# Exchanging the two arms of a run-time branch at the end of a two-layer decoder kernel

## The chip, the core and the metric

The kernel runs on one core of a Trainium2 chip. A core has five engines, each with a queue of its own instructions: TensorE (PE: matrix products; its weight loads are shown as PEld), VectorE (DVE), ScalarE (ACT), GpSimd (POOL) and SyncE (SP), which here only issues transfers. A queue is worked off in order by a sequencer; engines wait for each other by semaphores. Sequencer work (branches, semaphore steps, register moves) is listed in the profile under the engine's name with a "q" behind it (SPq, DVEq). 16 DMA engines move data between the device's main memory and the on-chip memory, and also the instructions themselves.

The metric is the time of one execution in device microseconds, as the median of several. A profiled execution also gives the span, from the first to the last instruction of the program.

## The reference

Two decoder layers over x of 4 batches x 256 tokens x 256 features in float32, each sublayer followed by a residual sum and a layer norm:

```python
x = _layernorm(x + _L0_attn_ref(x, ...))    # sliding-window attention, 16 heads
x = _layernorm(x + _L0_xattn_ref(x, ...))   # attention to 1601 context rows
x = _layernorm(x + _L0_ffn_ref(x, ...))     # ternary weights, quantised activations
x = _layernorm(x + _L1_attn_ref(x, ...))    # causal attention, 16 heads
x = _layernorm(x + _L1_xattn_ref(x, ...))   # linear attention, gated
x = _layernorm(x + _L1_ffn_ref(x, ...))     # 2 of 8 experts for each token
```

The change lies behind the last of them. Each token goes to 2 of 8 experts, and the result is a weighted sum:

```python
weights = probs * mask          # softmax of 8 logits, the two largest kept
for e in range(E):
    h = jax.nn.silu(x @ w1[e]) * (x @ w3[e])
    out = out + h @ w2[e] * weights[:, e:e + 1]
```

and the last step of the program is the layer norm of x plus that sum.

## The kernel before

The whole program is written as a list of operations, each with the tiles it reads and writes; a planner (`weave`) orders them by estimated times and due places, and then emits them into the queues. The line numbers that profiles show are therefore mostly those of helpers: L408 emits every operation of VectorE, ScalarE and GpSimd, L271 and L278 the products and transposes, L285 the plain transfers, L1290 the scatters.

**The expert tiles.** Tokens are sorted into lists by expert at run time, padded to tiles of 128 rows. How many tiles there are depends on the data. `tile_table` computes which expert and which rows a tile has. Some tiles are worked early, while the last batch is still in its attention. The rest, `LATE` of them, come at the end: the first `LATE - RARE` always run, and the last `RARE` = 3 only if the lists are so unevenly filled that more tiles are in use. `tile_table` writes this as a number of 0 or 1 to the tile `more` (L1423), which each engine's sequencer loads into a register (L1547).

**The end of the usual path.** The last tiles that always run add their result for each batch to four accumulators `acc` in PSUM, by a product with a selection matrix `pick`; VectorE adds the results of earlier tiles, read back from `yd` in main memory into tiles `back`, to x (`entry`), and a product with the identity adds this to `acc`. Then `finish` makes the layer norm. For each batch of 256 tokens (two groups of 128 rows): VectorE's bn_stats and bn_aggr for mean and variance (`st`, `mv2`); GpSimd's two small operations for the inverse root (`rstd2`); VectorE's `nmr`; VectorE normalises the first group into `back`, ScalarE the second with one Identity activation; SP stores both to `out`. So four activations of ScalarE and four stores of 256 KB end the usual path.

**The rare branch.** After that, `rare_tiles` emits one `tc.Switch` over all five engines. Its flag is `more`. Arm 0 has no work of its own; arm 1 works the three rare tiles, adds them to `acc`, and calls `finish` again, which writes all of `out` once more. In the program every engine's queue holds, in this order: its last usual instruction; the steps of the switch (register moves and a branch that takes its distance from a register, L1722); arm 0; arm 1; the closing block. Each arm begins with a hint that names its exit (BRANCH_PREFETCH_HINT, L1548) and ends with an unconditional branch to the closing block. The framework counts semaphores up through the whole program, so an arm also holds steps that bring each engine's and each DMA lane's semaphore to the value that the other arm would leave. Such a step first waits for the value that the lane has when all its own transfers have landed, and then adds the difference. In arm 0 these are nine on SP (eight DMA lanes and one for its sequencer), two on PE, one each on the others.

**The closing block** (L1722 too, as the line of `weave` in the caller). SP makes twelve semaphore steps of two waits each, which together wait for every semaphore of the program: four steps for the scatters' lanes, eight for the plain transfers' lanes in turn, each with an engine's semaphore as the second. Then it drains and gives its sign. The other engines drain and give theirs; GpSimd counts four signs, releases all, clears the semaphores, and a second round of signs ends the program.

With the inputs of the reference the flag `more` is 0: the usual arm is taken.

Of the kernel before, what the change touches and what calls it, by code (L numbers as in the profile page):

```python
# [23 lines left out]
F32 = mybir.dt.float32  # L24
BF16 = mybir.dt.bfloat16
U32 = mybir.dt.uint32
I32 = mybir.dt.int32
AF = mybir.ActivationFunctionType
ALU = mybir.AluOpType
AX = mybir.AxisListType  # L30

P = 128
B, S, D = 4, 256, 256
T = B * S
# [6 lines left out]
NE, EI = 8, 512  # L41
# [144 lines left out]
class Loom:  # L186
# [79 lines left out]
    def mm(self, o, lhsT, rhs, start, stop, **kw):  # L266
        fns, outs, ins = self.cur
        outs.append(o)
        ins += [v for v in (lhsT, rhs) if isinstance(v, View)]
        fns.append(  # L270
            lambda: self.nc.tensor.matmul(real(o), real(lhsT), real(rhs), start=real(start), stop=stop, **kw)  # L271
        )
# [162 lines left out]
def decoder(ctx: ExitStack, tc: tile.TileContext, a: dict, out: bass.AP):  # L435
    nc = tc.nc
    k = Loom(tc)
# [33 lines left out]
    p5, p5w = linear.pool("p5", 2), linear.pool("p5w")  # L471
# [3 lines left out]
    p6 = work.pool("p6", 3)  # L475

    def bank(shape=(P, 512), dtype=F32, acc=False):
        return psB.tile(shape, dtype, "bank", free=True, acc=acc)

    def tiny(shape, tag, dtype=F32):  # L480
        return small.tile(shape, dtype, tag, free=True)
# [21 lines left out]
    def at_prio(*prio):  # L503
        k.prio = prio
# [106 lines left out]
    vs = []  # L611
    for i in range(2):
        v = p1w.tile((P, 3, H // 2, 2, 32), F32, f"v{i}")
# [624 lines left out]
    LATE = TILES - sum(EARLY)  # L1238
    LAST_TILES = 2
    RARE = NE // 2 - 1  # L1240
# [138 lines left out]
    def tile_table(n, before, last=False):  # L1379


        iotaN, start, nxt = state[4:]
        tag = len(tables)

        def some(w, name):
            return p5.tile((P, w), F32, f"{name}{tag}", bufs=1)

        nt = some(NE, "nt")
        k.vector.tensor_scalar(nt, nxt, 1.0 / P, (127.0 if last else -127.0) / 256.0, ALU.mult, ALU.add)
        k.vector.tensor_scalar(nt, nt, MAGIC, MAGIC, ALU.add, ALU.subtract)  # L1390
        st = start
        if before is not None:
            st = some(NE + 1, "st")
            k.vector.tensor_copy(st, start)
            k.vector.tensor_tensor(st[:, :NE], st[:, :NE], before, ALU.add)
        k.vector.tensor_tensor(nt, nt, st[:, :NE], ALU.subtract)
        upto = some(NE, "upto")
        k.vector.tensor_copy(upto, nt)
        for e in range(1, NE):
            k.vector.tensor_tensor(upto[:, e : e + 1], upto[:, e : e + 1], upto[:, e - 1 : e], ALU.add)  # L1400

        step = some(NE, "step")
        k.vector.tensor_tensor(step, st[:, 1:], st[:, :NE], ALU.subtract)
        k.vector.tensor_tensor(step, step, nt, ALU.subtract)
        past = p5.tile((P, n, NE), F32, f"past{tag}", bufs=1)
        k.vector.tensor_tensor(
            past,
            upto.unsqueeze(1).to_broadcast([P, n, NE]),
            iotaN[:, :n].unsqueeze(2).to_broadcast([P, n, NE]),
            ALU.is_le,  # L1410
        )
        ex, row = some(n, "ex"), some(n, "rowt")
        k.vector.reduce_sum(ex, past, axis=AX.X)
        k.vector.tensor_tensor(past, past, step.unsqueeze(1).to_broadcast([P, n, NE]), ALU.mult)
        k.vector.reduce_sum(row, past, axis=AX.X)
        k.vector.scalar_tensor_tensor(row, row, st[:, 0:1], iotaN[:, :n], ALU.add, ALU.add)
        tab = p5.tile((P, 2, n), I32, f"tab{tag}", bufs=1)
        k.vector.tensor_scalar(tab[:, 0], ex, float(NE - 1), None, ALU.min)
        k.vector.tensor_scalar(tab[:, 1], row, float(P), None, ALU.mult)
        tables.append(tab)  # L1420
        if last:
            more = p5.tile((P, 1), I32, "more", bufs=1)
            k.vector.tensor_scalar(more, upto[:, NE - 1 :], n - RARE + 0.5, None, ALU.is_gt)  # L1423
            return tab, more

        taken = some(NE, "taken")
        k.vector.tensor_tensor(taken, nt, upto, ALU.subtract)
        k.vector.tensor_scalar(taken, taken, float(n), 0.0, ALU.add, ALU.max)
        k.vector.tensor_tensor(taken, taken, nt, ALU.min)
        if before is not None:  # L1430
            k.vector.tensor_tensor(taken, taken, before, ALU.add)
        return tab, taken
# [78 lines left out]
        k.vector.tensor_tensor(slots, slots, slot, ALU.add)  # L1511
        scatter(yd, slots, y, 1.0, 2.0, "give", cleared)

    def finish(acc):

        for b in range(B):
            mv = tiny((P, 2, 2), "mv2")
            o = p6.tile((P, 2, D), F32, "back", bufs=4)
            for t in range(2):
                st = tiny((P, 6), "st")  # L1520
                k.vector.bn_stats(st, acc[b][:, t, :])
                k.vector.bn_aggr(mv[:, t, :], st)
            rstd = tiny((P, 2), "rstd2")
            k.gpsimd.tensor_scalar(rstd, mv[:, :, 1], 1e-5, None, ALU.add)
            k.gpsimd.tensor_tensor(rstd, rstd, mhalf, ALU.pow)
            nmr = tiny((P, 1), "nmr")
            k.vector.scalar_tensor_tensor(nmr, mv[:, 1, 0:1], -1.0, rstd[:, 1:2], ALU.mult, ALU.mult)
            k.vector.tensor_scalar(o[:, 0], acc[b][:, 0], mv[:, 0, 0:1], rstd[:, 0:1], ALU.subtract, ALU.mult)
            k.scalar.activation(o[:, 1], acc[b][:, 1], AF.Identity, scale=rstd[:, 1:2], bias=nmr)
            k.dma_start(out[b * S : (b + 1) * S, :].rearrange("(t p) d -> p t d", p=P), o)  # L1530

    def rare_tiles(tiles, tab, more, level, acc):

        spare = {}
        for v in (
            p5.tile((P, W), F32, "xg"), p6w.tile((P, 2, 2, EI), F32, "wt"), p6.tile((P, 2, P), F32, "xgT"),
            p6.tile((P, EI // P, P), F32, "eh"), p6.tile((P, D), F32, "ey"), p5.tile((P, 1), F32, "of", bufs=2),
            p6.tile((P, T // P, P), F32, "pick", bufs=LAST_TILES), p6.tile((P, 2, D), F32, "back", bufs=4),
            tiny((P, 2, 2), "mv2"), tiny((P, 6), "st"), tiny((P, 2), "rstd2"), tiny((P, 1), "nmr"),
            bank((P, 2, P)), bank((P, EI // P, P)), bank((P, EI // P, P)), bank((P, D)),  # L1540
        ):
            spare.setdefault(v.buf.group.tag, []).append(v)

        def emit():
            k.hold_order(False)
            engines = (nc.tensor, nc.vector, nc.scalar, nc.gpsimd, nc.sync)
            which = {e.engine: e.value_load(more.real()[0:1, 0:1], min_val=0, max_val=1) for e in engines}  # L1547
            for arm in tc.Switch(which, 2):  # L1548
                if arm:
                    for i in tiles:  # L1550
                        k.at_once = spare
                        expert_tile(i, tab, level, acc)
                    finish(acc)
                    k.at_once = None
            k.hold_order(True)

        k.op({None: (0.0, 2.5, emit)}, [*acc], [tab, more, w2], [v for vs in spare.values() for v in vs], after=[o for o in k.ops if o.bufs], unordered=True)


    for b in range(B):  # L1560
# [40 lines left out]
    state, taken = moe_prepare(), None  # L1601
# [4 lines left out]
    w2 = p6w.tile((P, NE, 4, D), F32, "w2e")  # L1606
    for e in range(NE):
        k.dma_start(w2[:, e], rows(a["w2"][e]))
    level = 0
    for b in range(B):  # L1610
        at_prio(7, b)
        for ts, x, xt in l1_attention(b):
            at_prio(6, b)
            if ts[0] == 0:
                entry, xnt = new_entry(), new_xt()
                xn = entry[:, :, 0, :D]
            l1_cross(b, ts, x, xt, xn, xnt)
            if b == B - 1:
                at_prio(8)
                n = EARLY[ts[0]]  # L1620
                tab, taken = tile_table(n, taken)
                for i in range(n):
                    expert_tile(i, tab, level)
            at_prio(6, b)
            route(b, ts, entry, xnt, level)
            level += 1
            at_prio(7, b)
        X[b] = xn
    at_prio(8)
    tab, more = tile_table(LATE, taken, True)  # L1630
    iotaT = p6.tile((P, T), F32, "iotaT", bufs=1)
    iota(iotaT, 1, base=1)
    acc = [bank((P, 2, D)) for _ in range(B)]
    sure = LATE - RARE
    for i in range(sure):
# [5 lines left out]
        if last == 0:  # L1641
            for b in range(B):
# [6 lines left out]
                with piece(0.87, what="base"):  # L1649
                    for t in range(2):  # L1650
                        mm(acc[b][:, t, :], ident, x[:, t, :], False, True, skip_group_check=True)
    finish(acc)
    rare_tiles(range(sure, LATE), tab, more, level, acc)
    k.weave()


# [69 lines left out]
```

## Time and profile before

| what | value |
|---|---|
| median of 3 runs | 690.63 us (690.26 to 690.64) |
| the profiled execution's own time | 690.3 us |
| its span | 688.6 us |
| mean granted clock of TensorE | 0.985 |
| PE busy | 656.5 us (95% of the span) |
| DVE, ACT, POOL busy | 444.0, 296.2, 120.7 us |
| last product of TensorE ends | 675.0 us |
| last instruction of ScalarE | 678.88 us, 0.56 us long |
| stores of `out` issued | four, 675.4 to 679.5 us |
| their time from issue to landing | 3.2 / 4.1 / 4.5 us (least, median, most) |
| instruction packets of the DMA queues | 38 (0.62 MB) on q8, 37 (0.30 MB) on q14 |

Times within the profile count from the start of the span. The table says that TensorE is busy nearly all the time up to 675 us, and that some 13 us of the span lie behind its last product.

### The profile page before, as it was taken

The page shows a single profiled execution, that of the slowest core. Times are in us where ns is not written, and L with a number is a line of the kernel's source. Part 1 is how long each engine was busy: PE and PEld are TensorE (multiplying, and loading weights), DVE is VectorE, ACT ScalarE, POOL GpSimd, SP SyncE. Part 2 cuts the span into 40 slices and gives each one's busy share as a digit, 9 for nine tenths or more (in the row PEclk, how much of TensorE's full clock was granted, in tenths as well). Part 3 has the DMA queues.
Part 4 walks back from the last instruction along what each step waited for, and adds up shares of the span by engine and source line. Part 5 has one row for each costly group of instructions (what it writes and reads, how often), then busy time and mean ns, then how long its engine had stood idle before and what let it go on. Part 6 is the DMA issues. An engine that isn't in the chain of part 4 may idle for free.

```text
span 688.6 us, 12316 instructions
## 1 busy us (share of the span) xinstructions
PE 656.5 (95%) x4385; PEld 524.3 (76%) x4389; DVE 444.0 (64%) x1152; ACT 296.2 (43%) x930; POOL 120.7 (18%) x166
## 2 busy tenths in 40 slices
PE   9999999999999999999989999999997899999992
PEld 6778788678877777777667677777765799899991
DVE  6899887433526844464699997777688466434353
ACT  4779766211132423334347777656445312111101
POOL 3331132122300000000022101141203213121102
PEclk9999999999999999999999999999999899999996
DMA  9932121537998422000010340000000582895432
GB/s 307 363 96 63 45 66 40 177 100 236 335 340 307 146 96 96 0 1 1 1 54 1 105 142 1 1 32 1 31 1 21 207 277 73 295 339 217 146 130 69
DMA packets 62463, 85.36 MB, mean 124 GB/s; under 512 B 4462, under 2 KB 45812, under 8 KB 62388
## 3 DMA queue, kind: packets, MB, share of 16 engines
q1 hardware_dynamic: 60756, 79.96, 34.9%
q0 software_dynamic: 1632, 4.48, 1.8%
q8 instruction: 38, 0.62, 0.4%
q14 instruction: 37, 0.30, 0.1%
HBM read 67.29 MB, written 17.13 MB: 123 GB/s over the span
## 4 chain that ended last, share of the span: by engine, by line
PE 83%; DVE 10%; ACT 4%; POOL 1%; issue 1%; ACTq 0%; POOLq 0%; DVEq 0%
PE bank L271 74%; PE bank L278 9%; ACT at L408 3%; DVE at L408 2%; DVE nm L408 2%; DVE x L408 1%; POOL rstd L408 1%; DVE st L408 0%; DVE h L408 0%; DVE fm L408 0%; DVE as L408 0%; DVE kf L408 0%; ACT fm L408 0%; DVE back L408 0%; DVE bank L408 0%
## 5 line engine op out<-in xcount | busy, mean ns | idle before, releaser
L408 ACT ACTIVATE at<-at,nm 128x128 f32<-128x128 f32 (+1 forms) x256 | 106.4, 419 | 22.6 <-DVE nm L408 21.7
L271 PE MATMUL bank<-xgT,wt 128*128 128x128 f32 x640 | 75.9, 280 | 0.6 <-DVE xgT L408 0.5
L271 PEld LDWEIGHTS bank<-xgT,wt 128*128 128x128 f32 x640 | 75.2, 196 | 1.7 <-DVE xgT L408 0.8
L278 PE MATMUL bank<-ident,at 128*128 128x128 f32 (+1 forms) x440 | 61.4, 277 | 2.0 <-DVE at L408 1.8
L278 PEld LDWEIGHTS bank<-ident,at 128*128 128x128 f32 (+1 forms) x440 | 50.7, 142 | 14.2 <-issue 7.1
L271 PE MATMUL bank<-V,aT 128*128 128x256 f32 (+1 forms) x240 | 55.1, 380 | 0.6 <-DVE o L408 0.6
L271 PE MATMUL bank<-KT,qT 128*128 128x512 f32 (+1 forms) x128 | 54.7, 554 | 0.0
L271 PEld LDWEIGHTS bank<-V,aT 128*128 128x128 f32 (+1 forms) x240 | 45.3, 190 | 10.5 <-issue 3.6
L271 PE MATMUL bank<-kf,V 128*128 128x256 f32 (+1 forms) x208 | 50.0, 382 | 1.1 <-DVE kf L408 1.1
L408 POOL TENSOR_SCALAR rstd<-mv 128x2 f32<-128x2 f32 (+1 forms) x26 | 5.8, 222 | 258.5 <-DVE mv L408 186.2
L408 DVE TENSOR_REDUCE nm<-at 128x4 f32<-128x512 f32 (+1 forms) x64 | 50.6, 809 | 0.4
L271 PE MATMUL bank<-wkv,KT 128*128 128x256 f32 (+1 forms) x208 | 49.6, 382 | 0.0
L408 ACT ACTIVATION_READ_ACCUMULATOR at<-at,nm 128x1 f32 x256 | 48.6, 190 | 0.0
L271 PEld LDWEIGHTS bank<-kf,V 128*128 128x128 f32 (+1 forms) x208 | 38.6, 190 | 7.2 <-DVE kf L408 2.3
L271 PEld LDWEIGHTS bank<-wkv,KT 128*128 128x128 f32 (+1 forms) x208 | 38.0, 186 | 6.9 <-issue 1.0
L408 ACT COPY aT<-bank 128x512 f32<-128x512 f32 (+2 forms) x58 | 30.6, 554 | 26.6 <-PE bank L278 25.8
L408 ACT ACTIVATE eh<-bank 128x512 f32<-128x512 f32 x20 | 11.9, 597 | 66.5 <-PE bank L271 66.5
L408 DVE TENSOR_REDUCE m<-bank 128x1 f32<-128x512 f32 (+1 forms) x32 | 20.5, 640 | 29.7 <-PE bank L271 29.7
L408 DVE TENSOR_TENSOR at<-at,rs 128x512 f32<-128x512 f32 (+1 forms) x44 | 38.4, 873 | 1.0
L408 POOL TENSOR_TENSOR at<-at,rs 128x512 f32<-128x512 f32 (+1 forms) x20 | 22.8, 1141 | 87.9 <-DVE rs L408 80.7
L408 ACT ACTIVATE fm<-bank 128x512 f32<-128x512 f32 (+2 forms) x33 | 17.8, 550 | 46.6 <-PE bank L271 46.1
L271 PE MATMUL bank<-w2e,eh 128*128 x160 | 37.8, 380 | 0.0
(268 smaller groups left out, 1243.2 us busy)
## 6 DMA issues: line engine op xcount, KB each, us to landing
wt<-in_w SPq DMA_DIRECT2D x40, 512.0 KB, 5.0
lists<-h SPq DMA_DIRECT2D x6, 1548.0 KB, 17.9
KT<-in_ctxT SPq DMA_DIRECT2D x6, 1024.0 KB, 6.9
V<-in_ctx SPq DMA_DIRECT2D x6, 1024.0 KB, 6.0
w2e<-in_w SPq DMA_DIRECT2D x8, 512.0 KB, 8.7
KT<-in_ctxT SPq DMA_DIRECT2D x6, 577.0 KB, 5.1
V<-in_ctx SPq DMA_DIRECT2D x6, 512.0 KB, 4.2
xg<-lists SPq DMA_DIRECT2D x20, 129.0 KB, 4.2
```

The lines of the kernel that those rows point to most:

```text
L271: lambda: self.nc.tensor.matmul(real(o), real(lhsT), real(rhs), start=real(start), stop=stop, **kw)
L278: fns.append(lambda: self.nc.tensor.transpose(real(o), real(x), real(ident)))
L408: return getattr(engine, method)(*[real(x) for x in args], **{k: real(x) for k, x in kw.items()})
```

## The change

The flag is turned round: `enough` is 1 where the tiles that always run suffice. `finish` is split in two. `norms` has what VectorE and GpSimd do, and runs ahead of the switch as before; `leave` has the four activations of ScalarE and the four stores. The switch's arm 0 now holds the three rare tiles, then `norms` and `leave` again; arm 1, which stands last and directly ahead of the closing block, holds only `leave`. The rare arm writes the same tiles `back`, `rstd2` and `nmr` that the usual path has filled (entered in `spare`, but no longer claimed as places of their own), and the operation of the switch names them as written. The list of engines in the switch has another order.

```diff
         if last:
-            more = p5.tile((P, 1), I32, "more", bufs=1)
-            k.vector.tensor_scalar(more, upto[:, NE - 1 :], n - RARE + 0.5, None, ALU.is_gt)
-            return tab, more
+            enough = p5.tile((P, 1), I32, "enough", bufs=1)
+            k.vector.tensor_scalar(enough, upto[:, NE - 1 :], n - RARE + 0.5, None, ALU.is_lt)
+            return tab, enough
...
-    def finish(acc):
+    def norms(acc):
+        parts = []
         for b in range(B):
             mv = tiny((P, 2, 2), "mv2")
-            o = p6.tile((P, 2, D), F32, "back", bufs=4)
...
+            o = p6.tile((P, 2, D), F32, "back", bufs=4)
             k.vector.tensor_scalar(o[:, 0], acc[b][:, 0], mv[:, 0, 0:1], rstd[:, 0:1], ALU.subtract, ALU.mult)
+            parts.append((o, rstd, nmr))
+        return parts
+
+    def leave(acc, parts):
+        for b, (o, rstd, nmr) in enumerate(parts):
             k.scalar.activation(o[:, 1], acc[b][:, 1], AF.Identity, scale=rstd[:, 1:2], bias=nmr)
             k.dma_start(out[b * S : (b + 1) * S, :].rearrange("(t p) d -> p t d", p=P), o)

-    def rare_tiles(tiles, tab, more, level, acc):
+    def end(tiles, tab, enough, level, acc, parts):
...
+        held = [v for vs in spare.values() for v in vs]
+        for vs in parts:
+            for v, tag in zip(vs, ("back", "rstd2", "nmr")):
+                spare.setdefault(tag, []).append(v)

         def emit():
             k.hold_order(False)
-            engines = (nc.tensor, nc.vector, nc.scalar, nc.gpsimd, nc.sync)
-            which = {e.engine: e.value_load(more.real()[0:1, 0:1], min_val=0, max_val=1) for e in engines}
+            engines = (nc.tensor, nc.vector, nc.gpsimd, nc.sync, nc.scalar)
+            which = {e.engine: e.value_load(enough.real()[0:1, 0:1], min_val=0, max_val=1) for e in engines}
             for arm in tc.Switch(which, 2):
+                k.at_once = spare
                 if arm:
+                    leave(acc, parts)
+                else:
                     for i in tiles:
-                        k.at_once = spare
                         expert_tile(i, tab, level, acc)
-                    finish(acc)
-                    k.at_once = None
+                    leave(acc, norms(acc))
+                k.at_once = None
             k.hold_order(True)
...
-    finish(acc)
-    rare_tiles(range(sure, LATE), tab, more, level, acc)
+    end(range(sure, LATE), tab, enough, level, acc, norms(acc))
     k.weave()
```

In the built program the order of VectorE's, GpSimd's and TensorE's instructions ahead of the switch is the same as before. On ScalarE the switch follows the last activation of the expert tiles, on SP the eighth load of `back`. In the usual arm SP's queue has: the hint; for each of the four stores a step that brings its DMA lane forward, and the store; then five more steps (its sequencer and the four other lanes); the branch to the closing block. ScalarE's has the hint, the four activations with the steps that wait for their inputs, and the branch. VectorE, GpSimd and TensorE have in it what they had in arm 0 before. The rare arm has 57 instructions on VectorE and 117 (118 before) on TensorE, each product counted once.

## The prediction

> **What bounds the kernel now.** I read the page first, its span and its chain.
>
> ```profile
> span 688.6 us, 12316 instructions
> ...
> PE 83%; DVE 10%; ACT 4%; POOL 1%; issue 1%; ACTq 0%; POOLq 0%; DVEq 0%
> ```
>
> TensorE sets nearly everything, but the change touches only what follows its last product. So I read next the timeline of the last stretch. Columns: start, duration, engine, line, operation.
>
> ```profile
> 673.11 1.89 PE L271 MATMUL bank<-ey,pick 128*128 128x256 f32 x8
> 675.41 4.44 SPq L285 DMA_DIRECT2D out<-back  x4
> 678.26 0.54 DVE L408 TENSOR_SCALAR back<-bank,mv,rstd 128x256 f32<-128x256 f32 x1
> 678.88 0.56 ACT L408 ACTIVATE back<-bank,nmr,rstd 128x256 f32<-128x256 f32 x1 [0.42 <-DVE back L408]
> ```
>
> The products end at 675.0, ScalarE's last activation at 679.44, the fourth store is issued at 679.47. The span ends at 688.6: 9.1 us in which no engine computes. What fills them is in the rows of the switch (L1722, the closing block included) and of its first arm (L1548). First and last start stand behind the durations in ns.
>
> ```profile
> L1722 SPq EVENT_SEMAPHORE  x14: 17/28/28, 686.9 to 688.5; - x14
> ...
> L1722 POOLq DRAIN  x3: 40/112/2933, 681.2 to 688.3; - x3
> ...
> L1722 PEldq COMPARE_BRANCH  x2: 351/2010/3670, 672.2 to 675.3; - x2
> ...
> L1722 POOLq COMPARE_BRANCH  x2: 43/52/60, 677.6 to 678.3; - x2
> ...
> L1722 DVEq COMPARE_BRANCH  x2: 60/68/75, 678.4 to 679.2; - x2
> ...
> L1722 ACTq COMPARE_BRANCH  x2: 43/50/58, 679.1 to 679.7; - x2
> ...
> L1722 SPq COMPARE_BRANCH  x2: 42/50/58, 680.1 to 684.2; - x2
> L1722 DVEq DRAIN  x2: 10/29/48, 684.1 to 688.0; - x2
> L1722 ACTq DRAIN  x2: 8/44/80, 684.4 to 688.0; - x2
> ```
>
> Each queue branches twice: at the switch, into arm 0, which stands right behind; and out of arm 0, past the rare arm, to the closing block. SP's second branch is at 684.2 and its first closing semaphore step at 686.9: 2.7 us with nothing done. DVE's takes 679.2 to 684.1, 4.9 us; ACT's 679.7 to 684.4, 4.7; POOL's 678.3 to 681.2, 2.9; PE's 3.67 by its own duration. The first branch costs little: on DVE 678.4 to the arm's first record at 679.0, 0.6.
>
> Why SP leaves so late stands in the rows of arm 0 and in the waits of SP's queue (line, releaser, us in total, times, longest):
>
> ```profile
> L1548 SPq EVENT_SEMAPHORE  x9: 17/17/17, 680.7 to 684.2; - x9
> ```
> ```profile
> SPq L1548 <- SPq L1548: 3.0, 2, 1.6
> ```
>
> Arm 0 makes nine semaphore steps on SP. Each waits for its lane's last transfer before it adds what the rare arm would have added. Two of the lanes carry the third and the fourth store, so SP waits 3.0 us for them to land (682.6 and 684.0) and only then branches.
>
> Last, the DMA rows of 684.1 to 688.6, when no data move: the packets of the instruction queue, 8 KB each.
>
> ```profile
> q14 instruction: 4, 0.03, 2.5%
> ```
>
> So code is fetched while the queues stand at those branches. I read the long branches as fetches of code that was not there; the first branch is short because arm 0 follows in sequence.
>
> **The change part by part.** *The numbers of `norms` and the flag.* The same instructions in the same order on VectorE, GpSimd and TensorE; `enough` costs what `more` did, one tensor_scalar on one element. Cost 0, nothing need hide it.
>
> *ScalarE's activations and SP's stores move into arm 1.* ScalarE meets the switch after its last tile activation (659.43 + 0.60 = 660.0), SP after the eighth load of `back` (its last of L285 before the stores ends at 661.23 + 6.97 = 668.2). Both now take a far branch there. Priced by the rows above at 2.7 to 4.9 us, ACT stands in arm 1 by 664.9 and needs it at 674.8; SP, with 0.3 us of register steps, by 673.4 and needs it at 675.4. Slack 9.9 and 2.0 us: cost 0. Without that cover the first store would slip; only the last one counts, and it has 6.1 us. In the arm, ACT's waits ahead of each activation are on the same engines and lanes as before, and SP's four added steps (0.07 us each) stand ahead of stores that wait for ACT anyway. Queued behind them are only the next activation and store. The fourth store is issued at 679.47 as before.
>
> One collision remains: SP's fetch at 668.5 falls among the last loads of `back`, whose sum VectorE begins at 671.16 and TensorE reads at 672.25. An 8 KB packet takes 0.3 to 0.7 us at the tail; bounds 0 to +0.5, I take 0, because the sum of 0.67 us ends at 671.83 and leaves 0.4 of slack.
>
> *The nine steps of SP's arm lose their waits for the stores.* In the built program arm 1 brings forward the lanes of the stores ahead of the stores; behind the last one stand five steps on lanes that are long done, 0.07 us each: SP leaves the arm at about 680.3, not 684.2. The store's landing is then awaited in the closing block, whose tenth of twelve steps (0.06 us each) it is.
>
> *SP's far exit.* The closing block now stands right behind the arm in which SP has been since 673. By the short row it costs 0.6, by the long ones 2.7 to 4.9: there by 680.9 to 685.2. I take the short end, as arm 0 was near because it followed. Even 2.7 lies under the landing at 684.0.
>
> The sum, from the landing. Before: 684.03 to the end at 688.58, 4.55 us: 0.2 of last steps, 2.7 of branch, 1.65 of closing block. After: of the closing block only what follows the tenth step, 687.50 to 688.58, 1.07. Gain 4.55 - 1.07 = 3.5 us; span 688.6 - 3.5 = 685.1.
>
> *The other queues must be there in time.* SP would give its sign at 684.03 + 0.25 = 684.3, and GpSimd closes when all have. PE: 672.2 + 3.7 into arm 1, 0.3, 3.7 out: 679.9. ACT: last activation 679.4, exit at most 4.9 from its last issue at 678.9: 683.8. DVE: switch 678.4, far branch. Its 4.9 came when the branch followed 0.2 us after entry into an arm, with the arm's own fetch under way; SP and POOL, with 2.7 and 2.9, are nearer to a branch out of old code. I take 2.7: 681.1, 0.2 for the two steps, then the next block, which is the one in sequence: between 0.1 and a whole fetch of 2.7: 681.4 to 684.1. POOL: 677.6 + 2.9 + 0.2 = 680.7, exit 0.1 to 2.7, then its drain, 2.93 before (681.2 to 684.1): 683.7 to 686.3. I take the short exit for both, nearest to the row of code in sequence. All are then there by 684.3, narrowly.
>
> *The landing itself.* The four stores took 3.2 to 4.5 us; the slow one was the last, while four queues fetched code. ACT's and SP's far fetches now come earlier. Bounds: 4.5 to 3.2, that is 0 to -1.3; I take 0, since POOL and DVE still fetch, and with the POOL row above not more than 0.6 of it could be had.
>
> [...]
>
> **Against the runs.** The profiled execution took 690.3 us, 1.7 around its span; the median is 690.63, 0.33 above. Gain 3.5 from the median: 687.1 to 687.2; I say 687.2.
>
> **Rivals.** *A late queue takes the store's place.* POOL's exit costs a whole fetch and its drain stays: 686.3 at GpSimd's count, which was 687.8 before; gain 1.5, 689.1. It decides once POOL's or DVE's drain ends behind 684.3. For it: 4.9 us rows for branches soon after entry. Against: the closing block is now next in sequence.
>
> *The wait is hidden anyway.* If SP's exit from arm 1 were fetched only after the landing, or POOL and DVE both came at 687 to 688, nothing would move: 690.6 within 1.3. For it: hints stood in arm 0 too (BRANCH_PREFETCH_HINT, SP at 680.6), 3.6 us ahead of the branch, and did not shorten it. Against: SP no longer waits in front of its branch.
>
> *Slower.* GpSimd, last of all, pays two far branches at the dearest row in turn: 677.6 + 4.9 + 0.2 + 4.9 = 687.6, drain 2.9: 690.5, against 687.8 before: +2.7, 693.3. It decides where POOL's second branch ends behind 684.9. Against: its row is 2.9, not 4.9.
>
> *It doesn't do what it says*: a flag with the wrong sense would run three tiles on top. `more` and `enough` compare the same whole count with the same half: exact opposites, under 1 in 100.
>
> **How the numbers follow.** The store's landing sets the end: 0.66, 686.2 (landing shorter by 0.6, and by 0.3 more if the drain is short as well) to 687.7 (collision of 0.5). Late queue 0.20, 687.7 to 689.2. Nothing moves 0.09. Slower 0.05. The range 686.2 to 689.2 leaves out the last two and some of the first. A measurement here can tell about 0.2%, 1.4 us, from no change: faster means below 689.25: 0.66 + 0.19 = 0.85; same 0.10; slower 0.05.
>
> **What would show it.** In the changed profile SP's closing steps begin near 681, not 686.9, and only their tenth waits; ACT's and SP's switch branches lie near 660 and 668; the fourth store is still issued at 679.5; the last drains of DVE and POOL end before 684.3. It is wrong if the first `out` store is issued after 675.9, if DVE's or POOL's drain ends later than SP's closing steps, or if a fetch still lies between SP's last data and its closing steps.

## The result and the profile after

| | before | after |
|---|---|---|
| median of 14 runs each | 690.46 us (688.42 to 692.31) | 689.84 us (687.39 to 691.47) |
| ratio after to before | | 0.9991, 95% interval 0.9978 to 1.0004 |
| profiled execution: own time, span | 690.3, 688.6 us | 687.61, 685.9 us |

So 0.6 us were gained, with an interval from 1.5 gained to 0.3 lost; 3.5 were forecast. The profiled execution alone would mislead: it is 2.7 us shorter than the one shown of before, but 1.87 of these lie ahead of the first load of `back` (issued at 659.36 us, in the profile of before at 661.23); of what the change moves, only ScalarE's branch, at 657.7, comes earlier. Over all profiled executions of this study, whatever the kernel, that moment lies between 658.6 and 663.3. So times are given from here on relative to two fixed points: the issue of the eighth load of `back`, and the issue of the fourth store of `out`.

The timeline of the end after the change (start, duration, engine, line, operation):

```profile
674.34 4.36 SPq L285 DMA_DIRECT2D out<-back  x4
677.74 0.56 ACT L408 ACTIVATE back<-bank,nmr,rstd 128x256 f32<-128x256 f32 x1 [0.42 <-DVE back L408]
```

The fourth store is issued at 678.33. From there to the end of the span are 7.57 us, 9.11 before. The rows of the switch and the closing block (now L1733) and of the usual arm (L1557) say what fills them; first and last start stand behind the durations in ns:

```profile
L1733 SPq EVENT_SEMAPHORE  x18: 17/28/28, 669.7 to 685.8; - x18
...
L1733 SPq DRAIN  x3: 7/7/13, 681.2 to 685.3; - x3
L1733 POOLq DRAIN  x3: 40/113/2927, 682.1 to 685.6; - x3
...
L1733 ACTq COMPARE_BRANCH  x2: 43/50/58, 657.7 to 677.8; - x2
...
L1733 SPq COMPARE_BRANCH  x2: 42/47/52, 666.6 to 679.1; - x2
...
L1733 PEldq COMPARE_BRANCH  x2: 3435/3989/4543, 671.1 to 675.0; - x2
...
L1733 POOLq COMPARE_BRANCH  x2: 43/56/70, 676.5 to 679.5; - x2
...
L1733 DVEq COMPARE_BRANCH  x2: 60/68/75, 677.3 to 680.4; - x2
L1733 ACTq DRAIN  x2: 14/78/142, 678.2 to 685.3; - x2
...
L1733 DVEq DRAIN  x2: 10/29/48, 683.0 to 685.4; - x2
```
```profile
L1557 SPq EVENT_SEMAPHORE  x5: 17/17/17, 678.7 to 679.0; - x5
...
L1557 ACTq BRANCH_PREFETCH_HINT  x1: 46/46/46, 660.2 to 660.2; - x1
L1557 SPq BRANCH_PREFETCH_HINT  x1: 40/40/40, 669.6 to 669.6; - x1
...
L1557 POOLq BRANCH_PREFETCH_HINT  x1: 52/52/52, 679.3 to 679.3; - x1
...
L1557 DVEq BRANCH_PREFETCH_HINT  x1: 61/61/61, 680.2 to 680.2; - x1
```

Read along each queue. A way in is counted from the branch at the switch to the arm's first record, an exit from the arm's branch to the next record of the closing block. SP leaves the arm at 679.1 and drains for its sign at 681.2, once the last store has landed. ScalarE leaves at 677.8 and drains at 678.2: 0.45 us for the exit. GpSimd takes the switch at 676.5 and shows the arm's first record at 679.3 (2.9 us), leaves at 679.5 and starts its drain at 682.1 (2.6 us more); the drain takes 2.93 and ends at 685.05. VectorE: 677.3 to 680.2, 680.4 to 683.0.

The waits of SP's queue (line, releaser, us in total, times, longest) show the same from the other side:

```profile
SPq L1733 <- PEq L1733: 4.5, 2, 4.0
...
SPq L1733 <- DMA out<-back: 0.9, 2, 0.6
```

The second line is the wait for the stores, now in the closing block. The first is SP after its sign, waiting 4.0 us for the release. The profile names another queue's sign as releaser; the release is GpSimd's, and from 683.0 on, when VectorE has drained, GpSimd's drain is the only thing of the program still under way.

### The profile page after: what moved, and what is told of

It reads as the page before. It is cut to its first block, busy times and chain, and to the rows that moved or that the text cites. A ratio compares the mean times of both kernels' runs of the same rounds, so it can differ in the third digit from the quotient of the medians.

```text
span 685.9 us, 12319 instructions
## 1 busy us (share of the span) xinstructions
PE 653.6 (95%) x4389; PEld 521.0 (76%) x4389; DVE 443.6 (65%) x1152; ACT 296.2 (43%) x930; POOL 121.0 (18%) x166
## 4 chain that ended last, share of the span: by engine, by line
PE 78%; DVE 13%; ACT 4%; DMA 1%; issue 1%; POOL 1%; SPq 0%; DVEq 0%; POOLq 0%; ACTq 0%
PE bank L271 70%; PE bank L278 9%; DVE at L408 3%; ACT at L408 3%; DVE nm L408 2%; DVE x L408 1%; POOL rstd L408 1%; DVE as L408 1%; DVE h L408 1%; DMA wt<-in_w 1%; DVE st L408 1%; DMA back<-yd 1%; DVE entry L408 1%; DVE fm L408 0%; DVE hq L408 0%
```

## The experiments

All nine variants and the two repeats are put beside each other at the end of this section.

**Both kernels again, one execution each.** No edit.

> The kernel before, unchanged, for a second profile. Two stretches of the tail are compared in every run: A, from the issue of the eighth load of back to the issue of the fourth store (11.6 us in the first profile of before, 12.4 in that of after), and C, from the issue of the fourth store to the end of the span (9.1 before, 7.5 after). Theory (the change costs 0.7 in A, because SP's code fetch holds up one load, and gains 1.6 in C): A 11.6 and C 9.1 again, within 0.3. Rival (both differences are chance of one execution): A or C moves by 0.7 or more between two profiles of the same kernel. GpSimd's drain in the closing block 2.9 us again.

> The changed kernel, unchanged, for a second profile. Theory: A 12.4 and C 7.5 within 0.3, GpSimd's drain 2.9 us long and the last thing that ends before the signs are counted, VectorE's drain some 2 us ahead of it, SP's sign some 4 us ahead. Rival (chance): A near 11.6, or another engine than GpSimd last.

Measured: 688.14 and 689.36 us. From the fourth store to the end 8.95 us before (9.11 in the first profile) and 8.81 after (7.57). After the change GpSimd's drain ends last both times; in the repeat its entry and exit took 3.7 and 3.0 us, not 2.9 and 2.6. For the changed kernel the expectation that this stretch repeats within 0.3 us so failed, and the 1.5 us that the first profile shows behind the fourth store are the good end of a spread.

**GpSimd outside the branch.** The rare arm takes its root with VectorE and ScalarE instead (that arm isn't taken with these inputs; nothing is left out).

```diff
-    def norms(acc):
+    def norms(acc, pool=True):
...
+            if pool:
                 k.gpsimd.tensor_scalar(rstd, mv[:, :, 1], 1e-5, None, ALU.add)
                 k.gpsimd.tensor_tensor(rstd, rstd, mhalf, ALU.pow)
+            else:
+                k.vector.tensor_scalar(rstd, mv[:, :, 1], 1e-5, None, ALU.add)
+                k.scalar.activation(rstd, rstd, AF.Sqrt)
+                k.vector.reciprocal(rstd, rstd)
...
-            engines = (nc.tensor, nc.vector, nc.gpsimd, nc.sync, nc.scalar)
+            engines = (nc.tensor, nc.vector, nc.sync, nc.scalar)
...
-                    leave(acc, norms(acc))
+                    leave(acc, norms(acc, False))
```

> GpSimd is taken out of the switch: it goes straight from its last rstd to the closing block. The rare arm makes its roots on ScalarE and VectorE; that arm isn't taken here. Theory (GpSimd's two far branches, 2.9 and 2.6 us, and its drain of 2.9 set the end of the changed kernel): C falls from 7.5 to 5.4, set by VectorE's drain (4.6 us after the fourth store's issue, and 0.75 for the signs); time 2.1 us under the changed kernel's 689.8, so about 687.7, ratio to before 0.996. Rival 1 (the drain of 2.9 us is a cost of its own, whatever comes ahead): GpSimd's drain stays 2.9 us, but begins and ends 5 us earlier, C 5.4 all the same. Rival 2 (VectorE or SP sets the end and GpSimd only looks late): C stays 7.5 and the time 689.8. A stays 12.4 under all.

Measured: 686.97 us, ratio 0.9961 (0.9945 to 0.9977). The rows of its closing block:

```profile
L1738 POOLq DRAIN  x3: 45/108/3467, 675.5 to 682.9; - x3
L1738 SPq DRAIN  x3: 7/7/13, 680.5 to 682.6; - x3
...
L1738 DVEq COMPARE_BRANCH  x2: 60/68/75, 676.4 to 679.9; - x2
...
L1738 DVEq DRAIN  x2: 10/29/48, 682.3 to 682.6; - x2
```

GpSimd's long drain now starts at 675.5 and is over at 679.0. SP gives its sign at 680.5; the last to come is VectorE, whose exit at 679.9 leads to its drain at 682.3: 2.4 us. GpSimd's two branches were the cause of most of what was missing, and VectorE's are next.

**SyncE's fetch kept out of the loads.** A transfer of one element, to a scratch place that nothing reads, makes SP wait for the last load before it branches.

```diff
+    probe = in_dram((1, 1), "probe")
...
+                    if b == B - 1 and e:
+                        k.dma_start(probe, y[0:1, 0, 0:1])
```

> One transfer of 4 bytes is added on SP ahead of its switch; it reads what the eighth load brought, so SP takes its far branch only when all loads have landed. Theory (SP's fetch packet held up one of 16 engines' share of the seventh load, 0.9 us, and TensorE and VectorE waited for it): A falls from 12.4 to 11.6, VectorE's longest wait for a load from 1.25 to about 0.7 us, C stays 7.5, time 0.7 us under 689.8, about 689.1. SP stands in its arm 3 us after the load, ahead of the first store. Rival 1 (the loss in A has another cause, or is chance): A stays 12.4 and the time too. Rival 2 (SP now comes late): the first store is issued later than 8.5 us after the eighth load, A 12.4 or more, time 690 or more.

Measured: 690.11 us, ratio 0.9994 (0.9978 to 1.001), which is what the changed kernel has. The stretch from the eighth load to the fourth store was 11.65 us in its profile, against 12.37 and 12.10 in the two of the changed kernel; the time does not show it, though an interval of 1.1 us to each side could hide the 0.7 us that were expected.

**A hint for the switch, far ahead.** Each engine announces the switch when it has loaded the flag, 85 to 98 us before the fourth store.

```diff
-            for arm in tc.Switch(which, 2):
+            ahead_of = tc.switch_hint(which, 2)
+            for arm in tc.Switch(which, 2, hint=ahead_of):
```

> The changed kernel with a prefetch hint for the switch, on all five engines, placed where the flag is loaded, some 100 us ahead. Theory (the far branch waits for a fetch of code, which a hint in good time makes ahead): the branch into the arm falls from 2.5 to 3.4 us to 0.6 or less on every engine; no fetch among the loads, so A 11.7 instead of 12.1 to 12.4; GpSimd's and VectorE's exits still 2.6 to 3.0, so C falls from 8.2 (7.6, 8.8 and 8.6 so far) by 2.3 to about 5.9; time 2.7 under the changed kernel's, about 687.2. Rival (a hint is overwritten by the fetches in sequence that follow it, as the hint in the first arm of before, 3.6 us ahead of SP's exit, shortened nothing): entries stay 2.5 to 3.4, A 12.2, C 8.2, time 689.8.

Measured: 689.74 us, ratio 0.9978 (0.9961 to 0.9995). Its rows of the switch and of the arm:

```profile
L1734 POOLq COMPARE_BRANCH  x2: 56/62/68, 678.9 to 681.7; - x2
...
L1734 DVEq COMPARE_BRANCH  x2: 63/73/83, 679.7 to 680.5; - x2
...
L1734 DVEq DRAIN  x2: 10/38/65, 683.0 to 688.3; - x2
```
```profile
L1558 DVEq BRANCH_PREFETCH_HINT  x1: 45/45/45, 680.3 to 680.3; - x1
...
L1558 POOLq BRANCH_PREFETCH_HINT  x1: 40/40/40, 681.5 to 681.5; - x1
```

VectorE is in the arm 0.6 us after its branch (2.9 without the hint); its exit still takes 2.5. GpSimd's way in, 678.9 to 681.5 (2.6 us), stays near the 2.9 us without a hint, and GpSimd still ends the program. The expected 687.2 us were missed by 2.5, since they counted on a short way in for GpSimd too.

**Hint, and GpSimd outside.** Both edits above.

```diff
-            engines = (nc.tensor, nc.vector, nc.gpsimd, nc.sync, nc.scalar)
+            engines = (nc.tensor, nc.vector, nc.sync, nc.scalar)
...
-            for arm in tc.Switch(which, 2):
+            ahead_of = tc.switch_hint(which, 2)
+            for arm in tc.Switch(which, 2, hint=ahead_of):
...
-                    leave(acc, norms(acc))
+                    leave(acc, norms(acc, False))
```

> The hint and GpSimd outside the switch together. Theory: VectorE's drain at the fourth store's issue + 2.4 (4.9 without the hint), SP's sign at 3.1, so SP's landing of the stores sets the end: C 3.9, A 11.7, time 686.97 - 1.8 - 0.3 = 684.9. Rival (the hint does nothing): C 5.7, A 12.0, time 687.0 as with GpSimd outside alone.

Measured: 686.84 us, ratio 0.9939 (0.9918 to 0.996). From the fourth store to the end 4.75 us; SP's sign, 3.95 us behind the fourth store, comes last. Here the end is what was forecast for the change: the landing of the store. It took 3.7 us, so this stretch is longer than the 3.9 us expected, the one before it stayed at 12.12 us, not 11.7, and the time misses its 684.9 us.

**The old order of the arms.** The stores and ScalarE's activations are moved into the usual arm, but that arm stays first.

```diff
-            k.vector.tensor_scalar(enough, upto[:, NE - 1 :], n - RARE + 0.5, None, ALU.is_lt)
+            k.vector.tensor_scalar(more, upto[:, NE - 1 :], n - RARE + 0.5, None, ALU.is_gt)
...
-                if arm:
+                if not arm:
                     leave(acc, parts)
```

> Half of the change: the last activations and stores stand in the usual arm, but the arms have their old order, the usual one first, the rare one behind it. Theory (the gain comes from moving the stores into the arm alone, and the exchange of the arms costs: it gives GpSimd, VectorE and TensorE two fetches where they had one): branch into the arm 0.6 or less on every engine, so no fetch among the loads and A 11.7; exits from the usual arm 2.7 to 4.9, GpSimd's drain ends 4.6 us after the fourth store's issue, VectorE's too, SP's sign at 4.4: C 5.5; time 690.1 - 3.5 = 686.6, some 3 under the changed kernel. Rival (the exchange is what brings the gain, since SP's exit is then near): SP's exit behind the stores is far again, 4.9 or more, and C is 8.5 or more, time 689.5 or more.

Measured: 687.52 us, ratio 0.995 (0.9934 to 0.9966): half of the change is better than the whole. Its rows:

```profile
L1733 POOLq DRAIN  x3: 40/113/2927, 681.1 to 685.3; - x3
L1733 SPq DRAIN  x3: 7/7/13, 684.6 to 684.9; - x3
...
L1733 SPq COMPARE_BRANCH  x2: 42/50/58, 668.0 to 680.2; - x2
...
L1733 POOLq COMPARE_BRANCH  x2: 43/52/60, 677.5 to 678.2; - x2
```
```profile
L1557 SPq BRANCH_PREFETCH_HINT  x1: 40/40/40, 668.5 to 668.5; - x1
```

The short way in brings GpSimd's drain to its end at 684.1, and SP ends the program instead: it leaves at 680.2, pays a far exit of 3.7 us, finds the stores landed and gives its sign at 684.6.

**Old order, and GpSimd outside.** The edit of the last experiment, and:

```diff
-            engines = (nc.tensor, nc.vector, nc.gpsimd, nc.sync, nc.scalar)
+            engines = (nc.tensor, nc.vector, nc.sync, nc.scalar)
...
-                    leave(acc, norms(acc))
+                    leave(acc, norms(acc, False))
```

> The old order with the stores in the usual arm, and GpSimd outside the switch. Theory (VectorE and GpSimd end level in the old order, so one alone brings little): C 5.4 by VectorE, A 11.7, time within 0.4 of the old order with GpSimd inside, about 686.4. Rival (GpSimd's drain is last there too): C 4.5, time a further 1 us down.

Measured: 686.11 us, ratio 0.992 (0.9893 to 0.9947). SP's sign, 4.50 us behind the fourth store, comes last, not VectorE's as expected.

**Hint, GpSimd outside, SyncE held back.** The kernel with hint and GpSimd outside, with the small transfer again:

```diff
+    probe = in_dram((1, 1), "probe")
...
+                    if b == B - 1 and e:
+                        k.dma_start(probe, y[0:1, 0, 0:1])
```

> The kernel of e6 (hint far ahead, GpSimd outside the branch) with e4's small transfer, which keeps SyncE before its branch until the last load has landed. Theory (SyncE's code arriving among the last loads costs up to half a microsecond of the loop's end, and nothing else of it is on the path): the stretch from the issue of the eighth load to the issue of the fourth store falls from 12.1 us to about 11.7, the stretch after the fourth store stays near 4.8 us, and the time is 0.4 to 0.5 us under e6's 686.84: 686.4, a ratio of 0.993 to the kernel before. Rival (the collision is worth nothing that lasts): the first stretch stays at 12.1 and the time is e6's. Second rival (SyncE, late at its branch, now ends last): the second stretch grows to 6 us or more and the time is 688.0 or above, 0.996.

Measured: 686.79 us, ratio 0.9934 (0.9918 to 0.995). The first stretch was 12.03 us, not 11.7, though SP now came to its branch behind the loads: the expectation failed, and the rival (worth nothing that lasts) stands.

**The whole of `norms` in the usual arm.** VectorE and GpSimd then stay in the arm, GpSimd from a time at which it waits anyway. In `norms` the last two steps of a batch come behind the next batch's statistics, and each batch has tiles of its own.

```diff
-                    leave(acc, parts)
+                    leave(acc, norms(acc))
...
-    end(range(sure, LATE), tab, enough, level, acc, norms(acc))
+    end(range(sure, LATE), tab, enough, level, acc)
```

> The changed kernel with the whole of norms moved into the usual arm too, so that VectorE and GpSimd take the switch before their last work and stand in the arm for some 7 us and 18 us, not 0.2. GpSimd takes it while it waits for its first mean anyway. Theory (a branch out of an arm costs a whole fetch only to a queue that has just come in): VectorE's and GpSimd's exits cost 0.3 to 0.6 us, not 2.5 and 2.6; GpSimd's drain stays 2.9 us long and ends some 4 us earlier against the fourth store than in the changed kernel, 0 to 1 us behind it; SyncE's sign for the store's landing ends the program, the stretch behind the fourth store is 4.0 to 4.9 us. The price stands in the stretch before: VectorE pays its far switch (2.9 us) between its last sum and its first statistic, which it now begins some 3 to 4 us later, so that stretch grows from 12.2 us to 15 or 16. Sum 19 to 20.5 us against 20.5 in the changed kernel, ratio to the kernel before 0.997 to 0.999. Rival (these exits cost 2.5 us whatever the queue did before): VectorE's branch out of the arm to its drain takes 2.5 us again and GpSimd's too, the stretch behind the fourth store is 5 us or more.

Measured: 688.26 us, ratio 0.9965 (0.9946 to 0.9985). Its rows:

```profile
L1736 POOLq DRAIN  x3: 45/118/3174, 681.5 to 686.9; - x3
...
L1736 POOLq COMPARE_BRANCH  x2: 43/56/70, 658.6 to 681.0; - x2
...
L1736 DVEq COMPARE_BRANCH  x2: 60/64/69, 672.0 to 681.8; - x2
...
L1736 PEldq COMPARE_BRANCH  x2: 3620/4259/4898, 672.8 to 676.9; - x2
...
L1736 DVEq DRAIN  x2: 19/48/76, 682.4 to 686.6; - x2
```
```profile
L1561 POOLq BRANCH_PREFETCH_HINT  x1: 52/52/52, 661.3 to 661.3; - x1
...
L1561 DVEq BRANCH_PREFETCH_HINT  x1: 61/61/61, 674.9 to 674.9; - x1
```

GpSimd leaves at 681.0 and drains at 681.5 (0.46 us by the records), VectorE leaves at 681.8 and drains at 682.4 (0.57), out of the same arm into the block behind it as in the changed kernel, where they paid 2.6 and 2.5. What differs is how long they had been in it (20 and 7 us, not 0.2), and that the arm now holds more instructions for them. TensorE, which still only passes through, pays 4.9, in the changed kernel 4.5 and 5.4. The stretch behind the fourth store is 4.03 us; the price is VectorE's far way in, and the stretch before grew to 15.33.

**The same with the hint.**

```diff
-            for arm in tc.Switch(which, 2):
+            ahead_of = tc.switch_hint(which, 2)
+            for arm in tc.Switch(which, 2, hint=ahead_of):
```

> e10 with the hint far ahead of the switch (as in e5), which had shortened VectorE's switch to 0.4 to 0.6 us. Theory: exits short as in e10, the stretch behind the fourth store 4.0 to 4.9 us, and the stretch before it 12.5 to 13.3: together 17 us against 20.5 in the changed kernel; ratio to the kernel before 0.994 to 0.996. Rival: exits of 2.5 us, the stretch behind the fourth store 5 us or more.

Measured: 686.82 us, ratio 0.9945 (0.9926 to 0.9965). Stretches 12.91 and 3.80 us; GpSimd's exit 0.44, VectorE's 0.53.

The runs side by side. The first two columns are us from the eighth load's issue to the fourth store's, and from there to the end, each in one profiled execution. "Tail's gain" is 20.78 (the mean sum of the two executions of before) less the sum of the two. The measured gain is (1 - ratio) times the median of before on that chip.

| kernel | load to store | store to end | ends last | tail's gain | measured gain (95%) |
|---|---|---|---|---|---|
| before, twice | 11.63, 11.87 | 9.11, 8.95 | SP | 0 | |
| after, twice | 12.37, 12.10 | 7.57, 8.81 | GpSimd's drain | 0.8, -0.1 | 0.6 (-0.3 to 1.5) |
| SP's fetch kept out | 11.65 | 8.63 | GpSimd's drain | 0.5 | 0.4 (-0.7 to 1.5) |
| hint | 12.34 | 8.04 | GpSimd's drain | 0.4 | 1.5 (0.3 to 2.7) |
| GpSimd outside | 11.97 | 5.73 | VectorE | 3.1 | 2.7 (1.6 to 3.8) |
| hint, GpSimd outside | 12.12 | 4.75 | SP, landing | 3.9 | 4.2 (2.8 to 5.7) |
| the same, SP held back | 12.03 | 4.42 | SP, landing | 4.3 | 4.6 (3.5 to 5.7) |
| old order | 12.02 | 6.14 | SP, exit | 2.6 | 3.5 (2.4 to 4.6) |
| old order, GpSimd outside | 12.33 | 5.30 | SP, exit | 3.1 | 5.5 (3.7 to 7.4) |
| `norms` in the arm | 15.33 | 4.03 | SP, landing | 1.4 | 2.4 (1.0 to 3.7) |
| the same, hint | 12.91 | 3.80 | SP, landing | 4.1 | 3.8 (2.4 to 5.1) |

In all rows but one the tail's gain lies within the interval of the measured one. In the old order with GpSimd outside it is 0.5 below; why that kernel is that much faster stays open. It and the three with a hint and 4.75 us or less behind the last store have the lowest ratios, and their intervals lie wholly below 1 and below that of the changed kernel; but these four intervals overlap each other, so none is called best.

## Why the prediction was wrong

The failed step stands under "The other queues must be there in time": "I take the short exit for both, nearest to the row of code in sequence." The closing block being next in sequence did not make the exits of VectorE and GpSimd short. They cost 2.5 and 2.6 us in the first profile, up to 3.4 for GpSimd in the later ones. GpSimd's drain so ended 6.7 to 8.0 us behind the fourth store and set the end. That is the first rival, "a late queue takes the store's place", with its price: it put GpSimd's end 6.8 us behind the store (686.3 less 679.47) and the gain at 1.5 us, which is what the first profile has there (9.11 - 7.57); the other executions came out dearer, and the medians show 0.6. The forecast left 5.6 us behind the fourth store (9.11 - 3.5); the two profiles of the changed kernel have 8.2 on the mean, which is 2.6 of the 2.9 us that are missing.

*The place of the target alone did not make an exit short; the time in the arm went with it.* In the changed kernel ScalarE and SP, 17.5 and 9.6 us in the arm, pay 0.45 and 0.44 us; GpSimd, VectorE and TensorE, 0.2 to 0.4 us in it, pay 2.6, 2.5 and 4.5. The run with `norms` in the arm shows it by an intervention: the same two queues, let in early, pay 0.46 and 0.57. And time alone wasn't enough: in the old order SP stands 11.7 us in its arm, with its target past the rare arm, and pays 3.7. I had the rows for it in hand, the 4.9 us of branches soon after an entry among them, and judged by the place. One of them I read wrongly: GpSimd's 2.9 us was called "nearer to a branch out of old code", but in the profile of before GpSimd too had entered its arm only 0.2 us ahead of that branch (678.1 to 678.3).

The packets of the instruction queue fit this. In the changed kernel's profile, two 8 KB packets start near each of the two early entries: at 658.69 and 661.30 us around ScalarE's (its arm's first record is at 660.22), at 667.84 and 670.13 us around SP's (669.56). The second of each pair has run 1.9 and 1.0 us after the entry; GpSimd's and VectorE's exit branches come after 0.2. In the run with `norms` in the arm GpSimd leaves from 681.0 to 681.5, and no 8 KB packet runs between 676.1 and 682.1 us. Which queue a packet serves and what code it brings is not shown; and since the arm with `norms` also holds more code, time and code were not varied apart. SP with the small transfer had been 6.1 us in the last arm and left it in 0.43 us.

*SP's chain: right.* Its exit took 0.44 us (0.6 was the row used); its closing steps began 1.2 us behind the fourth store (1.4 by the forecast); only the steps with the stores waited, 0.9 us in all.

*The far ways in of ScalarE and SP: right.* 2.5 and 3.0 us, both done before their first work was due. The activations and stores did not slip for them.

*The landing: a term of the wrong size, but not on the path.* The last store landed 2.66 us after its issue (3.54 in the repeat), 4.55 before; I took no change and at most 0.6 less. With GpSimd last this bought nothing.

*The collision of SP's fetch with the loads: not settled, and small.* I took 0 within 0 to 0.5. The waits of the changed kernel's profile show a longer stall of VectorE on a load (1.2 us, on the sixth) than before (0.7), and TensorE standing behind it:

```profile
DVE entry L408 <- DMA back<-yd: 1.9, 2, 1.2
...
PEld bank L271 <- DVE entry L408: 0.9, 1, 0.9
```

But four profiled executions without a packet of code at that place have 11.63 to 12.03 us in the first stretch (those of before, and the two with SP held back), and seven with one 11.97 to 12.37. (In the old order and with the hint it is the packet behind SP's entry, at 669.7 to 671.5 us.) That is 0.4 us between the means, with ranges that overlap. Neither time with SP held back differs from its twin's (0.9994 against 0.9991, 0.9934 against 0.9939). A few tenths are possible; nothing shows them to last.

*Nor was the exchange of the arms the part that pays.* The prediction read the gain as one thing. The runs split it: moving the stores into the arm gains 3.5 us in the old order already (ratio 0.995). The exchange gives SP its near exit (3.7 to 0.4 us) and takes the near way in from the three queues that only pass through: GpSimd from 0.5 to 2.9 us, VectorE from 0.6 to 2.9, TensorE from 0.4 to 3.4. GpSimd had no room for it.

## What to carry to other kernels

At a run-time branch, list for every engine the way in, the time in the arm, the way out and what must still follow, and count back from the end. An engine with no work in a far arm paid here for two branches in a row (2.9 and 2.6 us on GpSimd), so keep it out of the branch or let it in early, while it waits for something else. Before exchanging arms, try the half of the change that only shortens the path of the last engine.

## What the hardware showed that was not expected

- GpSimd's first drain at the end takes 2.9 us in all 13 profiles, from its own start or from the end of GpSimd's last operation: 2.93 when its last operation was 5 us past, and 3.47 or 3.17 when it was issued during that operation, which is again 2.9 behind the operation's end. In these kernels it is a fixed term on the path wherever GpSimd is late.
- A hint 76 to 95 us ahead of the branch cut the way into the far arm from between 2.5 and 3.6 us down to 0.4 to 0.6 on TensorE, VectorE, ScalarE and SP, but not on GpSimd, which still took 2.6 in both runs in which it had one. The hints that stand in the arms did not make the exits past the rare arm short: in the old order SP passes its own 11.7 us ahead of the branch and still pays 3.7, ScalarE 19.2 us ahead and pays 4.4.
- One share of a load came late where a packet of code ran. Each load of `back` lands in 16 shares. In the changed kernel's profile 15 of the seventh load's had landed by 668.16 us; the last one came at 669.03. An 8 KB packet of the instruction queue ran from 667.84 for 0.68 us, and packets of 1 KB resume where it ends, at 668.52, one every 0.042 us up to that share's end. The trace names no DMA engine, so it is not shown that the one held up the other. Nor did VectorE lose time by it: its sum of the seventh load began at 669.14, 0.61 us after that of the sixth, as two sums without a wait do (663.88 and 664.50). Its wait of 1.25 us, up to 668.53, was for the sixth load, whose last share landed at 668.43, 0.95 us behind the other 15 and while the packet of code still ran. A share also came late with no code about: in the second profile of before the last share of the third load came 1.0 us behind the other 15, and no packet of code ran between 654.6 and 671.6 us, while it landed at 664.1.
